# Pacing of indexed transfers, input and accumulator loads moved, and a reshuffled end of the last image

## The chip, the cores and the metric

The kernel runs on one core of a Trainium2 chip. The metric is device time in microseconds (us) of one execution. The engines are called as in the profile: PE is TensorE, DVE is VectorE, ACT is ScalarE, POOL is GpSimd, SP is SyncE (here it only issues DMAs).

## The reference, cut to what matters

The input is x of shape (4, 32, 128, 128). Layer 0 turns each image into 128 channels by 4096 positions. Layer 1 takes the result as 4096 tokens of 128 numbers per image.

```python
# layer 0, per image: q = xs is 128 channels (32 x 2 x 2) by 4096 positions
energy = einsum('bci,bcj->bij', q, q); d = sqrt(diagonal(energy))
attn = softmax(energy / (d_i * d_j))          # over positions
x = gamma * einsum('bcj,bij->bci', q, attn) + xs
# layer 1, on tokens t
t = t + linear_attention(layernorm(t))        # K^T V first, 8 heads
p = softmax(layernorm(t) @ router_w + router_b); top 2 of 8 experts, weights renormalised
t = t + sum over the two experts of weight * (layernorm(t) @ expert_w[e] + expert_b[e])
```

## The kernel before, in words

Four images (b = 0 to 3) go through one after another. The body of an image is `attend` (L387): for eight row chunks i of 512 positions and the chunks jc up to i, TensorE makes a 128x512 tile of energies (`pe`, L503), ScalarE takes its exponential and row sums (`pr`, L506), and TensorE multiplies it with the image into `po` (L410), two ticks later. The energy matrix is symmetric, so each tile off the diagonal serves twice: VectorE transposes it in 32x32 blocks (`F`, L361), SP stores it to DRAM (`blocks`, L453, 1 MB) and loads it back three ticks later with the blocks in place (`G`, L461, four loads), and TensorE multiplies it into `pg` (L367) when 57 units of work have passed; VectorE adds that to `o` (L377). For the last image's last row two tiles skip DRAM: 16 loads from F to G each (L446).

Beside the body of image b runs, in small steps, the rest: `prep` for image b + 1 (L278), `input_rows` for image b (L533, four loads of T from x per chunk, four chunks, on SP) and `layer1` for image b - 1 (L541). The lists `timed` and `steady` (L1213 to L1245) set the order: a `timed` entry has a begin and an end in per cent of the body's work, a `steady` one is advanced once for every 10 units of work. So one step of layer 1 comes about every three 128x512 products. Everything on PE, DVE, ACT and SP stays in the order in which the Python program emits it. What an engine waits for holds up everything after it on that engine.

In `layer1`, `close_rows` (L610) ends layer 0 for a quarter of the tokens (row sums, `pbd`, `df`, added into T), takes norm statistics, normalises into `xn` (ScalarE, L583, or VectorE, L666) and adds to the Gram matrix (`pgram`, L608). `matrix` (L684) turns the Gram matrix into one 128x136 matrix for attention (`pgv` L703, `pm` L711, `matx` L709). `attention_rows` (L791) applies it, stores the tokens to DRAM (t2) and routes. For images 0 to 2 `sorted_experts` (L832), once for each half h of the tokens, does the experts: GpSimd scatters tokens by expert with indexed DMAs (`xs`, L910), tiles of one expert are loaded (L933), transposed and multiplied (`pys`, L966 and L973), copied (L943 on ScalarE, L948 on VectorE) and stored (`ys`, L952); then GpSimd gathers two rows for each token (`yb`, L1028), and VectorE adds them, weighted (`combine`, L1000), into `acc`, which was loaded from t2 on SP (L1026), and `put` stores it (L1010). `acc` has three buffers of four token tiles. For image 2 five indexed transfers are issued in two steps, for images 0 and 1 four (L899, L918, L1033).

DMAs from SP and ACT also wait for the eighth DMA before them, since eight completion counters serve in turn.

The last image has no further body beside it. `first_parts` runs its `close_rows`, and `last_parts` (L1096) does the rest without sorting: all eight experts' products for each token tile k (`py`, L1107, two 128x512 products), VectorE adds some of the eight with the gate as weight (`scaled_sums`, L1055), ScalarE scales the others into `tmp` (`scaled_rows`, L1069), GpSimd sums these (`sum_rows`, L1076 to L1080), and `store` writes out. While the first half of the tokens goes through this, `second_half` (L1147) prepares the second half on the same engines, a piece at each k.

Of the kernel before, what the change touches and what calls it, by code (L numbers as in the profile page):

```python
# [22 lines left out]
def kernel(  # L23
# [156 lines left out]
    def idle(n):  # L180
        for _ in range(2 * n):
            yield

    held = []
    banks = [3]
# [92 lines left out]
    def prep(b, kc, st):  # L278
# [39 lines left out]
        for s in range(2):  # L318
# [8 lines left out]
            yield  # L327
        yield from idle(1)
        scaled = []
        for s in range(2):  # L330
# [56 lines left out]
    def attend(b, st):  # L387
# [11 lines left out]
        for i in range(NCH):  # L399
# [79 lines left out]
            for jc in order:  # L479
# [17 lines left out]
                for j in range(NJ):  # L497
                    t = NJ * jc + j
                    c0 = 0 if jc < i else P * j
                    yield  # L500
                    tick[0] += 1
                    pe = ps_e.tile([P, CH], F32, tag="pe", name=f"pe_{b}_{i}_{t}")
                    nc.tensor.matmul(pe[:, c0:], qn[jc][:, ts(j, P)], qn[i][:, c0:], start=True, stop=True)  # L503
                    pr = ppool.tile([P, CH], F32, tag="pr", name=f"pr_{b}_{i}_{t}")
                    exps[:] = [
                        nc.scalar.activation(pr[:, c0:], pe[:, c0:], AF.Exp, accum_out=sums[:, t, i : i + 1]).ins  # L506
                    ]
                    own.append(pr)
                    after(2, partial(values, pr[:, c0:], t, c0, CH))
                    if jc < i and not both:  # L510
                        after(1, partial(nc.vector.transpose, Fb[:, :, :, j, :], pr))
                        if j == NJ - 1:
                            after(2, partial(move, F, i, jc))
                    elif jc == i and j in (1, 2):

                        after(1 if j == 2 and order[-1] == i else 2, partial(below, own, (2, 1) if j == 1 else (3,)))
                    turn_tick()
                    clock[0] += 2 * (CH - c0) // P
                    step_share()
                    yield  # L520
# [20 lines left out]
    def layer1(b, st):  # L541
# [68 lines left out]
        def close_rows(kc):  # L610


            while len(st["o"]) < 2 * kc + 2 or any(st["got"][c] < NCH - 1 - c for c in (2 * kc, 2 * kc + 1)):
                yield from idle(1)
            late_rows = alone and kc >= 2
            while b > 0 and kc == 0 and not states[b - 1].get("sorted"):
# [28 lines left out]
            for j in range(NJ):  # L645
                nc.tensor.transpose(pb[:, ts(j, P)], wide[:, j].rearrange("p s c -> p (s c)"), ident)
            yield
            done()
            if not late_rows:
# [14 lines left out]
            if late_rows:  # L664
                for j in range(k + 4, k + 8):
                    nc.vector.tensor_scalar(  # L666
                        xn[:, j, :], T[:, j, :], rsa[:, j, :], nba[:, j, :], ALU.mult, ALU.add
                    )
            yield
            gram_rows(range(k, k + 4))  # L670
            yield
# [11 lines left out]

        def matrix(between=()):  # L684

# [20 lines left out]
            yield  # L706
            for f in between:
                f()
            pm, done = hold(f"pm_{b}", lambda p: nc.vector.tensor_copy(matx[:, : D + E], p[:, : D + E]))  # L709
# [122 lines left out]
        def sorted_experts(h):  # L832
# [65 lines left out]

            pause = (1, 4) if b == B - 2 else (1, 3)  # L899
            period = 5 if b == B - 2 else 4  # L900

            def offset(ap):
# [5 lines left out]
            for n in range(2 * HR):  # L908
# [9 lines left out]
                scatters.append(inst.ins)  # L918
                if n % period in pause:
                    yield  # L920
                    yield
# [75 lines left out]
            def combine(n):  # L997
# [5 lines left out]
                if k % 4 == 3 and i == 1:  # L1003
                    after_steps.append((now[0] + 2, partial(put, k // 4)))

            def put(g):
                for s in range(2):
                    for r1 in range(2):
                        p0 = s * 64 + r1 * 32
                        nc.sync.dma_start(dst_out[s, r1, :, ts(g, 4), :], accs[g][p0 : p0 + 32])  # L1010
# [11 lines left out]
            for n in range(2 * HR):  # L1022
                k, i = r0 + n // 2, n % 2
                if k % 4 == 0 and i == 0:
                    accs[k // 4] = work.tile([P, 4, D], F32, tag="acc", name=f"acc_{b}_{k // 4}", bufs=3)
                    nc.sync.dma_start(accs[k // 4], t2[:, ts(k // 4, 4)])  # L1026
                    yb[k // 4] = work.tile([P, 2, 4, D], F32, tag="wide", name=f"yb_{b}_{k // 4}")
# [3 lines left out]
                wait_for(pinned(inst).ins, exps, "not more of these at a time than steps have")  # L1031
                after_steps.append((now[0] + 3, partial(combine, n)))
                if n % period in pause:  # L1033
                    yield
                    yield
                    due()
# [23 lines left out]
        def scaled_rows(k, py, n=4):  # L1060

            if k % 2 == 0:
                nm = f"tmp_{b}_{k // 2}"
                if n == 4:
                    tmps[k // 2] = work.tile([P, 2, n, D], F32, tag="wide", name=nm)
# [8 lines left out]
        def sum_rows(kk, n=4, eng=nc.gpsimd):  # L1074
            tmp, rows = tmps[kk], accs[kk // 2][:, 2 * (kk % 2) : 2 * (kk % 2) + 2, :]
            eng.tensor_tensor(tmp[:, :, 0:2], tmp[:, :, 0:2], tmp[:, :, 2:4], ALU.add)  # L1076
            eng.tensor_tensor(tmp[:, :, 0], tmp[:, :, 0], tmp[:, :, 1], ALU.add)
            if n == 5:
                eng.tensor_tensor(rows, rows, tmp[:, :, 4], ALU.add)
            eng.tensor_tensor(rows, rows, tmp[:, :, 0], ALU.add)  # L1080
# [15 lines left out]
        def last_parts():  # L1096
# [3 lines left out]
            def bank(name):  # L1100
# [3 lines left out]
                return pool.tile([P, CH], F32, tag=tag, name=name)  # L1104

            def product(k, h, bank):
                nc.tensor.matmul(bank, xn[:, k, :], ew_sb[:, 4 * h : 4 * h + 4, :], start=True, stop=True)  # L1107
                return bank

            for _ in matrix([lambda g=g: transpose_rows(g)() for g in (6, 7)]):  # L1110
                pass

            la = fpool.tile([P, KT, 2 * E], F32, tag="F", name=f"la_{b}")
            copies = {}
            for u in range(4):
                if u >= 2:
                    copies[u] = fpool.tile([P, 8, D + 2 * E], F32, tag="F", name=f"pac_{b}_{u}")
                for j0 in range(0, 8, 3):
                    pa = bank(f"pat_{b}_{u}_{j0}")
                    attend_rows(u, j0, pa)  # L1120
                    if u < 2:
                        add_rows(u, j0, la[:, 8 * u : 8 * u + 8], pa)
                    else:
                        nj = min(3, 8 - j0)
                        nc.scalar.activation(
                            copies[u][:, j0 : j0 + nj].rearrange("p j d -> p (j d)"),
                            pa[:, : nj * (D + 2 * E)], AF.Copy,
                        )
            for u in (0, 1):
                bs, stats = batch_stats("f", 8 * u, 8)  # L1130
                for f in stats:
                    f()
                close_stats("f", 8 * u, 8, bs)
            logits = router_rows(nc.vector, 0, 16, la[:, :16])
            next(logits)
            normalise(range(0, 8), rsf, nbo)
            for _ in logits:
                pass
            gates = route(0)
            next(gates)  # L1140
            transpose_tokens(0)()
            transpose_tokens(1)()
            normalise(range(8, 16), rsf, nbo)
            for _ in gates:
                pass

            def second_half():  # L1147

                bs, stats = batch_stats("f", 16, 16)
                for u in (2, 3):  # L1150
                    tg = T[:, ts(u, 8), :]
                    nc.vector.tensor_tensor(tg, tg, copies[u][:, :, :D], ALU.add)
                    yield
# [4 lines left out]
                close_stats("f", 16, 16, bs)  # L1158
                for u in (2, 3):
                    nc.vector.tensor_copy(la[:, ts(u, 8)], copies[u][:, :, D:])  # L1160
                yield
                logits = router_rows(nc.vector, 16, 16, la[:, 16:])
                gates = None
                for g in range(4, 8):
                    normalise(range(4 * g, 4 * g + 4), rsf, nbo)
                    if g < 6:
                        next(logits, None)
                    else:
                        gates = gates or route(1)
                        next(gates, None)  # L1170
                    yield
                    transpose_tokens(g)()
                for _ in gates:
                    yield

            rest = second_half()
            products = [product(k, h, bank(f"py_{b}_{k}_{h}")) for k in range(2) for h in range(2)]
            transpose_tokens(2)()
            transpose_tokens(3)()
            for k in range(KT + 4):  # L1180
                if k < KT:
                    n = 5 if k < 16 else 4
                    scaled_sums(k, products[:2], 8 - n)
# [4 lines left out]
                if 1 <= k <= KT and k % 2 == 0:  # L1188
                    sum_rows(k // 2 - 1, 5 if k <= 16 else 4, nc.vector if k == KT else nc.gpsimd)
                if k >= 5 and k % 4 == 1:  # L1190
# [23 lines left out]
    for b in range(B):  # L1214
# [6 lines left out]
        if b + 1 < B:  # L1221
            nxt = states[b + 1]
            timed.append((prep(b + 1, 0, nxt), 66, 82, 12))
            timed.append((prep(b + 1, 1, nxt), 83, 99, 12))
        timed.append((input_rows(b, states[b]), 55, 75, 9))
        done = [0] * len(timed)
# [69 lines left out]
```

## Time and profile before

| | us |
|---|---|
| median of 3 runs (1788.23 to 1793.99) | 1790.51 |
| profiled execution, its own time | 1748.38 |
| its span, first to last instruction | 1746.6 |
| PE busy | 1666.0 |
| DVE busy | 878.6 |
| ACT busy | 929.6 |
| POOL busy | 509.2 |
| DMA | 330.81 MB, mean 189 GB/s |

All other times in this document's views come from the profiled execution and count from its first instruction. A wait line reads: engine and line that waited, what it waited for, us in total, number of times, longest. A timeline line reads: start, length, engine, line, operation, output<-input, count, and in brackets the idle time before it with what ended it; "x2" beside one 128x512 float32 product means its two passes, about 0.86 us together at the full clock. A window line reads: stretch, its length, busy time with the number of instructions, TensorE's granted clock (1 is full), share of the DMA engines, GB/s. The profile places the body of image 0 at about 0 to 400 us, image 1 at 400 to 800, image 2 at 800 to 1200 and image 3 at 1200 to 1637; the end of image 3 follows.

### The profile page before, as it was taken

How to read it: one execution, taken by the hardware profiler on the slowest of the kernel's cores; microseconds unless marked ns; L12 is line 12 of the kernel's file. 1: busy time of each engine (PE TensorE's matmuls, PEld its weight loads, DVE VectorE, ACT ScalarE, POOL GpSimd, SP SyncE). 2: the span in 40 equal slices, each digit the busy share in tenths (PEclk: the TensorE clock that was granted, in tenths of full speed). 3: DMA queues.
4: the chain of work that ended last, by engine and by line, in shares of the span. 5: the costliest groups of instructions: out<-in, count | busy, mean ns of one | idle time of the engine just before them, and what ended most of it. 6: DMA issues, size and time to landing. Idle time of an engine off the chain costs nothing. (4 is left out here: it accounts for less than half of the span.)

```text
span 1746.6 us, 20682 instructions
## 1 busy us (share of the span) xinstructions
PE 1666.0 (95%) x5580; PEld 891.6 (51%) x5580; DVE 878.6 (50%) x2213; ACT 929.6 (53%) x2875; POOL 509.2 (29%) x554
## 2 busy tenths in 40 slices
PE   7999999999999999989999999999999999989777
PEld 4544544455554556535564455544555455535533
DVE  3423333456385235556458334456647523444687
ACT  3555445465565545446565554545656554535376
POOL 1000000001026604651014630662101760562156
PEclk9999999999999999989999999999999999999999
DMA  2665788855657999884556889987555699984001
GB/s 63 169 186 164 214 210 246 234 162 145 178 156 217 256 247 258 251 246 114 148 170 198 247 236 254 267 251 199 145 156 170 209 271 256 271 253 108 1 13 37
DMA packets 217843, 330.81 MB, mean 189 GB/s; under 512 B 24448, under 2 KB 136576, under 8 KB 203776
## 3 DMA queue, kind: packets, MB, share of 16 engines
q1 hardware_dynamic: 200928, 296.82, 60.5%
q0 software_dynamic: 12288, 25.19, 5.0%
q10 hardware_dynamic: 4512, 7.48, 1.4%
q8 instruction: 46, 0.75, 0.2%
q14 instruction: 69, 0.57, 0.1%
HBM read 171.45 MB, written 160.96 MB: 190 GB/s over the span
## 5 line engine op out<-in xcount | busy, mean ns | idle before, releaser
L506 ACT ACTIVATE pr<-pe 128x512 f32<-128x512 f32 (+1 forms) x576 | 322.7, 560 | 553.9 <-PE pe L503 528.1
L410 PE MATMUL po<-pr,qT 128*128 128x512 f32 (+3 forms) x1152 | 550.4, 560 | 0.5 <-ACT o L415 0.5
L367 PE MATMUL pg<-G,qT 128*128 128x512 f32 x880 | 455.0, 599 | 25.4 <-DVE o L377 25.3
L503 PE MATMUL pe<-qn,qn 128*128 128x512 f32 x896 | 463.9, 600 | 1.8 <-ACT pr L506 1.8
L361 DVE STREAM_TRANSPOSE F<-pr 128x512 f32<-128x512 f32 x440 | 308.7, 704 | 196.8 <-ACT pr L506 195.0
L410 PEld LDWEIGHTS po<-pr,qT 128*128 128x128 f32 x1152 | 217.7, 191 | 243.7 <-issue 232.6
L372 ACT ACTIVATE junk<-G 128x512 bf16<-128x512 f32 x440 | 273.0, 620 | 0.0
L367 PEld LDWEIGHTS pg<-G,qT 128*128 128x128 f32 x880 | 162.8, 192 | 210.3 <-issue 156.9
L1028 POOL DMA_INDIRECT yb<-ys,place x192 | 185.0, 964 | 154.0 <-DMA ys<-xn 58.8
L910 POOL DMA_INDIRECT xs<-xn,place x192 | 185.9, 968 | 115.1 <-issue 39.0
L503 PEld LDWEIGHTS pe<-qn,qn 128*128 128x128 f32 x896 | 155.7, 192 | 117.4 <-issue 107.9
L377 DVE TENSOR_TENSOR o<-o,pg 128x512 f32<-128x512 f32 x110 | 75.1, 682 | 235.0 <-PE pg L367 234.7
L166 POOL TENSOR_TENSOR rn<-ss,neg_half 128x8 f32<-128x8 f32 (+1 forms) x17 | 26.8, 1578 | 459.7 <-DVE ss L321 401.4
L948 DVE COPY xn<-pys 128x256 f32<-128x256 f32 (+1 forms) x120 | 49.8, 416 | 187.1 <-ACT xn L943 106.3
L506 ACT ACTIVATION_READ_ACCUMULATOR pr<-pe 128x1 f32 x576 | 111.9, 194 | 0.0
L943 ACT ACTIVATE xn<-pys 128x256 f32<-128x256 f32 (+1 forms) x120 | 44.7, 377 | 115.2 <-PE pys L973 114.2
L1000 DVE SCALAR_TENSOR_TENSOR acc<-yb,weight,acc 128x128 f32<-128x128 f32 x192 | 64.7, 342 | 71.7 <-DMA yb<-ys,place 40.1
L166 POOL TENSOR_TENSOR rsf<-dm_f,neg_half 128x8 f32<-128x8 f32 (+1 forms) x15 | 26.1, 1743 | 255.0 <-DVE sv_f L575 255.0
L966 PEld LDWEIGHTS pys<-ew_sb,xn 128*128 128x128 f32 x468 | 69.8, 193 | 56.6 <-issue 45.1
L503 PE MATMUL pe<-qn 128*128 128x512 f32 (+3 forms) x256 | 91.4, 439 | 0.7 <-ACT qn L338 0.7
L166 POOL TENSOR_TENSOR rsa<-dm_a,neg_half 128x8 f32<-128x8 f32 x16 | 26.3, 1644 | 220.7 <-DVE sv_a L575 220.7
L372 ACT ACTIVATION_READ_ACCUMULATOR junk<-G 128x1 f32 x440 | 84.5, 192 | 0.0
(178 smaller groups left out, 1550.1 us busy)
## 6 DMA issues: line engine op xcount, KB each, us to landing
blocks<-F SPq DMA_DIRECT2D x108, 1024.0 KB
G<-blocks SPq DMA_DIRECT2D x432, 256.0 KB
xn<-xs SPq DMA_DIRECT2D x114, 128.0 KB
ys<-xn SPq DMA_DIRECT2D x114, 128.0 KB
T<-in_x_dram SPq DMA_DIRECT2D x64, 128.0 KB
out_dram<-acc SPq DMA_DIRECT2D x128, 64.0 KB
xx<-in_x_dram SPq DMA_DIRECT2D x62, 128.0 KB
t<-T SPq DMA_DIRECT2D x12, 512.0 KB
```

The costliest lines, as they stand in the source:

```text
L166: pinned(nc.gpsimd.tensor_tensor(dst, src, neg_half.to_broadcast(list(src.shape)), ALU.pow))
L361: f()
L367: nc.tensor.matmul(pg.rearrange("p (a f) -> p a f", a=4), st["qT"][i][:, ib, :], G[:, :, ib], start=(ib == 0), stop=(ib == NJ - 1),)
L372: nc.scalar.activation(junk, G[:, :, ib], AF.Copy, accum_out=st["sums"][:, NJ * i + ib, jc : jc + 1])
L377: nc.vector.tensor_tensor(o, o, pg.rearrange("p (a j c) -> p a j c", a=4, c=S), ALU.add)
L410: nc.tensor.matmul(row["po"][:, lo:hi], qT[blk // NJ][:, blk % NJ, :], w, start=start, stop=(row["left"] == 0))
L503: nc.tensor.matmul(pe[:, c0:], qn[jc][:, ts(j, P)], qn[i][:, c0:], start=True, stop=True)
L506: nc.scalar.activation(pr[:, c0:], pe[:, c0:], AF.Exp, accum_out=sums[:, t, i : i + 1]).ins
L910: inst = nc.gpsimd.indirect_dma_start(xs[h], offset(place[:, i, k : k + 1]), xn[:, k, :], None)
L966: nc.tensor.matmul(p[:, 2 * P + j * D : 2 * P + j * D + D], bufs[4 + g % 2][:, j, :], weights[:, bass.ds(begins[2 * (g % 2) + j], D)], sta ...
L1000: nc.vector.scalar_tensor_tensor(a[:, k % 4, :], yb[k // 4][:, i, k % 4, :], weight[:, i, k, :], a[:, k % 4, :], ALU.mult, ALU.add)
L1028: inst = nc.gpsimd.indirect_dma_start(yb[k // 4][:, i, k % 4, :], None, ys, offset(place[:, i, k : k + 1]))
```

## The change

1. `keep_running` issues transposes of the identity into a spare bank, whose result nobody reads: 22 at the first `prep`, 36 before the last quarter's Gram products, 6 before the first token transposes of the end.
2. In `sorted_experts` two indexed transfers are issued in each step for every image; images 0 and 1 had that already.
3. The load of `acc` goes from SP's queue to ACT's and is issued one step later; `combine` comes four steps after its gather instead of three.
4. `input_rows` of images 1 and 2 runs at 82 to 99 per cent of the body instead of 55 to 75.
5. The end of the last image: the last `close_rows` emits its row-sum work when the last exponential has been emitted, so that its `pbd` transposes come before the last `po` product; its Gram products are emitted in the order k, k+4, k+1, k+5 and so on; `transpose_rows` of groups 6 and 7 moves from before `pm` to after the first `pat`; statistics of the first eight tiles come before the second `pat`; ScalarE copies the logits' part `la`; the second half's first pieces come before the first gate; ScalarE takes 6 of the 8 scaled products for k under 8, 5 for k under 14, then 4 (before: 5 for k under 16, then 4), and the `tmp` tiles of 6 and 5 come from the pool of G with three buffers.

```diff
+    def keep_running(n, pool=None, tag=None):
+        bank = psum_t("spare") if pool is None else pool.tile([P, CH], F32, tag=tag, name="spare")
+        for _ in range(n):
+            nc.tensor.transpose(bank[:, :P], ident, ident)
...
         yield from idle(1)
+        if first:
+            keep_running(22, ps_y, "py")
         scaled = []
...
+            while "exps" not in st if last_rows else missing():
                 yield from idle(1)
...
                 nc.tensor.transpose(pb[:, ts(j, P)], wide[:, j].rearrange("p s c -> p (s c)"), ident)
             yield
+            while missing():
+                yield from idle(1)
             done()
...
+            if last_rows:
+                keep_running(36)
+                gram_rows([k + j // 2 + 4 * (j % 2) for j in range(8)])
+                yield
+                return
             gram_rows(range(k, k + 4))
...
-            pause = (1, 4) if b == B - 2 else (1, 3)
-            period = 5 if b == B - 2 else 4
...
-                if n % period in pause:
+                if n % 2:
                     yield
                     yield
...
+            def fetch(g):
+                nc.scalar.dma_start(accs[g], t2[:, ts(g, 4)])
...
-                    nc.sync.dma_start(accs[k // 4], t2[:, ts(k // 4, 4)])
+                    after_steps.append((now[0] + 1, partial(fetch, k // 4)))
...
-                after_steps.append((now[0] + 3, partial(combine, n)))
-                if n % period in pause:
+                after_steps.append((now[0] + 4, partial(combine, n)))
+                if n % 2:
...
-            eng.tensor_tensor(tmp[:, :, 0:2], tmp[:, :, 0:2], tmp[:, :, 2:4], ALU.add)
+            m = n // 2
+            eng.tensor_tensor(tmp[:, :, :m], tmp[:, :, :m], tmp[:, :, m : 2 * m], ALU.add)
...
+            def by_scalar(k):
+                return 6 if k < 8 else 5 if k < 14 else 4
...
-            for _ in matrix([lambda g=g: transpose_rows(g)() for g in (6, 7)]):
+            for _ in matrix():
                 pass
...
+            attended(0)
+            stats_of(0)
+            transpose_rows(6)()
+            transpose_rows(7)()
+            attended(1)
+            stats_of(1)
+            attended(2)
+            attended(3)
...
+            logits = router_rows(nc.vector, 0, 16, la[:, :16])
+            next(logits)
+            normalise(range(0, 4), rsf, nbo)
+            keep_running(6)
+            transpose_tokens(0)()
+            next(rest)
+            for _ in logits:
+                pass
+            gates = route(0)
+            normalise(range(4, 8), rsf, nbo)
+            next(gates)
+            next(rest)
+            for _ in gates:
+                pass
             products = [product(k, h, bank(f"py_{b}_{k}_{h}")) for k in range(2) for h in range(2)]
+            transpose_tokens(1)()
+            normalise(range(8, 16), rsf, nbo)
             transpose_tokens(2)()
             transpose_tokens(3)()
...
-        timed.append((input_rows(b, states[b]), 55, 75, 9))
+        timed.append((input_rows(b, states[b]), *((55, 75) if b in (0, B - 1) else (82, 99)), 9))
```

## The prediction

> **What bounds the kernel now.** I read the busy table, then TensorE's waits, then the stretches in which those waits lie, then VectorE's and SP's timeline there.
>
> ```profile
> PE 1666.0 (95%) x5580; PEld 891.6 (51%) x5580; DVE 878.6 (50%) x2213; ACT 929.6 (53%) x2875; POOL 509.2 (29%) x554
> PE pg L367 <- DVE o L377: 25.3, 13, 6.2
> PE pgram L608 <- ACT xn L583: 8.6, 2, 8.3
> PE pys L966 <- DVE xn L948: 8.3, 3, 4.0
> PE py L1107 <- ACT tmp L1069: 8.1, 5, 1.9
> PE ptn L340 <- DVE qs L332: 8.0, 3, 4.6
> ```
>
> TensorE is busy 1666.0 of 1746.6 us, and the change takes no matmul of use away. Only its 80.6 us of waits, and the slow clock that follows long ones, are for sale. TensorE waits for VectorE, though VectorE is half idle; so I looked at what VectorE waits for.
>
> ```profile
> 648.91 0.42 DVE L948 COPY xn<-pys 128x256 f32<-128x256 f32 x1 [9.18 <-DMA ys<-xn]
> 649.39 1.22 PE L966 MATMUL pys<-ew_sb,xn 128*128 x4 [4.04 <-DVE xn L948]
> ...
> 764.00 0.74 DVE L1000 SCALAR_TENSOR_TENSOR acc<-yb,weight,acc 128x128 f32<-128x128 f32 x2 [5.97 <-DMA acc<-t]
> 772.23 2.08 PE L367 MATMUL pg<-G,qT 128*128 128x512 f32 x2 [6.24 <-DVE o L377]
> ...
> 753.08 1.75 SPq L461 DMA_DIRECT2D G<-blocks  x4
> 754.92 1.86 SPq L1010 DMA_DIRECT2D out_dram<-acc  x4
> 756.99 0.34 SPq L1026 DMA_DIRECT2D acc<-t  x1
> ```
>
> Image 1's body holds two stalls. At 649 a copy waits for a ys store while the DMA engines run at a share of 1.0 to 1.2. At 764 VectorE waits for acc, which SP issued last, behind 1 MB of G and 256 KB of stores. Image 2's body repeats both (4.0 us at 1068, 6.5 us in 1100:1200). Image 3's has 9.7 us in 1450:1600, where VectorE waits 23.6 us for gathers (yb) and 24.3 us for ys stores.
>
> ```profile
> 1641.50:1642.00 0.50, 0.00 (x0) 0.87 0.00 0
> 1648.50:1649.00 0.50, 0.50 (x5) 0.80 0.00 0
> 1645.74 3.45 PE L608 MATMUL pgram<-xn 128*128 128x128 f32 x16 [8.28 <-ACT xn L583]
> ```
>
> These show TensorE's clock (last-but-two column) halve at 1641.9 in the 8.28 us wait and return at 1648.7, so 16 matmuls took 3.45 us where the 16 at 1633 took 1.95.
>
> **What the Trainium skill says.** (1) TensorE: Matmul & The Clock Gate, Part 1: activity is judged in free-running windows of about 3.4 us. The trace agrees: 1641.9, 1648.7, 1665.7 and 1672.6 lie whole multiples of 3.41 apart; a window about 77% busy (648.6 to 652.0) did not raise the clock, one 38% busy (764.7 to 768.1) lowered it. (2) The same page, Part 4, says that transposes don't engage the fast clock; no stretch of this trace is of transposes alone for a whole window, so it is open. (3) DMA: Bandwidth & Descriptors, Queues, rings and completion order: an engine turns between the rings of SP and ACT packet by packet, so a transfer on ACT's ring needn't sit out SP's backlog. No row here has acc on ACT. (4) SBUF — State Buffer, SBUF: two separate sides: a GpSimd operation and a VectorE one with two SBUF inputs shut each other out. It agrees: 128x128 router operations take 0.29 us alone and 0.70 to 1.39 beside GpSimd's sums (1693 to 1697).
>
> **The change, part by part.** A stall is priced as its wait plus half of the slow-clock time in which TensorE then worked.
>
> *T loads of images 1 and 2, from 55–75 to 82–99 per cent of the body.* They take 2.1 MB per image (about 8.4 us at the 250 GB/s of that stretch) and 16 SP issues out of 600 to 650. Stakes: 4.0 + 6.0/2 = 7.0 us (image 1), 4.0 + 3.3/2 = 5.7 (image 2). I take 10 of 12.7. They land in 730 to 775, before T is first read at 768.7, but that stretch already moves 242 GB/s: see below.
>
> *acc load on ScalarE's queue, a step later; combine a step later.* Distance load to use stays three steps. What goes is the place behind G and the stores: issue to landing was about 7 us (756.99 to 763.9). Stakes: 7.9 + 6.1/2 = 10.9 (image 1, 700:800), 6.5 + 3.2/2 = 8.1 (image 2). I take 13 of 19. What it adds: 24 issues on ScalarE of about 0.46 us (row of L204 at 2.2 us), hidden in its 1.28 us idle per step; and a wait. The load reuses the buffer of three groups before, so ScalarE, in order, waits for that group's stores, with the exponentials behind it, and TensorE behind those. Stores are issued four steps (4 x 2.58 = 10.3 us) before. They now follow a 1 MB blocks store, so they land perhaps 9 to 10 us after. TensorE's second next pe needs the exponential, so about 3.4 us of ScalarE delay is covered. The T loads delay G in the same place by 2 us a chunk. For both together I take 2 us loss per image, 4 in images 1 and 2 (bounds 0 and 15).
>
> *Two transfers per step for image 2.* One gather costs GpSimd 0.94 + 0.30 = 1.25 us, so 2.5 per step need 3.1 us where a step has 2.58; two need 2.5, which fits. Image 3's stakes are 9.7 + 3.5/2 = 11.4. The ys part remains, since image 3's T loads stay at 55–75: I take 5.5 (bounds 0 and 11.4). The phase ends later: 64 steps instead of 51, that is 33 us, with gathers until about 1605, where VectorE still has idle pieces of 7 to 8 us; cost nothing, at most 2 if that cover is gone. But stores of groups 3 and 4 now follow, on SP, the two rows of 16 G loads (13.4 and 10.9 us). I follow ScalarE's loads for groups 6 and 7: each waits about 5 us, less 3.4 covered; the second meets a ScalarE with normalising to do. I take 4 lost (bounds 0 and 9).
>
> *22 transposes at the start.* They fill 7.75 to 12.4, in which TensorE waits anyway; all slow they take 22 x 0.213 = 4.7 us, so at most 0.15 us late. If they raise the clock, the first ptn, pe and ptn save 0.45 + 1.05 + 0.45 = 2.0. Both ends kept; I take 1.5.
>
> *The end.* (a) pbd before the last po: df starts after o at about 1634.6 instead of 1636.54: 1.9. (b) 36 transposes (3.9 us) before the gram: if they count, up to 1.5 us of slow clock goes; if not, the earlier start gives 1 back: take 0.75. (c) ptx 6 and 7 leave the way of pm: 0.65. (d) From the first pat to the finished gate: 18.2 us before. After, counted through the new order (pat_0 adds, 8 statistics, close, 2.25 of GpSimd, second eight, router, the added T add of 1.22 and 4 statistics of 0.86, 14 route operations): 19.1. Loss 0.9, with 2.1 us of later VectorE work done. (e) From the gate to VectorE's end: 69.4 before. TensorE's floor is 30 x 1.72 + 7 x 0.43 = 54.6. VectorE gives six products to ScalarE; for k under 14 VectorE then has 29 us, ScalarE 31 (78 x 0.28, 4 normalisings of 1.65, 4 evictions), GpSimd 30, with a sum of 768 elements estimated at 1.9 us from 1.27 for 512. With three buffers for tmp this leaves about 39 us to k = 17, then 14 x 1.72 = 24, and 3.3 of closing: 67, gain 2.4. Sum 1.9 + 0.75 + 0.65 - 0.9 + 2.4 = 4.8 (bounds 0 and 8).
>
> **Sum:** 10 + 13 - 4 + 5.5 - 4 + 1.5 + 4.8 = 26.8 us off the profiled 1748.4 (span 1746.6 and 1.8 around it), to 1721.6. The median, 1790.51, lies 42 us above that execution; its extra time is not on the page, so I carry the gain over in us: 1763.7, say 1764.
>
> **Rivals.**
> - *Crowding eats the second gain.* The T loads join a stretch at 242 of some 260 GB/s; acc is prompt, but G and blocks are late, VectorE waits again. For: share about 1.0 for most of 740 to 790. Against: some 13 us of free DMA time in 740:800. Then the 13 goes: 1777.
> - *All stalls go*, being one chain that fed itself, and the end gains 8: 12.7 + 19 + 11.4 + 2 + 8 less about 8 of ScalarE's waits = 45: 1745.
> - *Slower: ScalarE waits for stores at each of 24 loads.* Without it the gain is about 35. It decides from 35/24 = 1.5 us a load beyond the 3.4 covered, a mean wait of 4.9 us. At 6 us: 24 x 2.6 = 62 lost, net 27 slower: 1818; at 5.2 us about 1799.
> - *It does nothing:* stalls move to the next DMA wait, transposes don't count, the end evens out: 1790.
>
> **Chances.** Forecast (1754 to 1770) 0.47, crowding (to 1785) 0.22, all stalls 0.15, nothing 0.07, slower 0.09. A measurement tells 0.3% (5.4 us) from no change. Faster 0.84, same 0.07, slower 0.09. The range 1740 to 1787 leaves out the slower case and the far end of the third.
>
> **What would show it.** Right: no wait of VectorE for acc on 700:800 and 1100:1200; no 9 us wait for ys near 649 and 1066; few yb waits after 1540; PE waits under pg L367 below 12 us; clock 1.0 from about 10.3 us and at the last gram. Wrong: ScalarE idle before an exponential on acc or stores; G named before pg; slow clock through the transposes.

## The result and the profile after

| | before | changed |
|---|---|---|
| median of 4 runs, side by side, us | 1792.25 (1788.23 to 1794.64) | 1767.69 (1764.09 to 1771.84) |
| profiled execution, its own time, us | 1748.38 | 1771.84 |

The ratio is 0.9866, interval 0.9836 to 0.9896: 24.6 us faster, where 26.8 were forecast. A set here is a group of runs timed side by side. The two profiles can't be subtracted: before has a median of 1751 us in two sets (its profile shown above is of that kind) and of 1790 to 1800 in the others, even on one chip, so each comparison below is made inside one set, with the time of before in that set beside it. Three single executions of the third set, 2514 to 5167 us long, are left out of its ratios.

TensorE's busy line of the changed kernel:

```profile
PE 1681.7 (95%) x5644; PEld 896.6 (51%) x5644; DVE 878.2 (50%) x2199; ACT 928.2 (52%) x2893; POOL 510.3 (29%) x553
```

64 transposes are new in it (5644 - 5580). Its `pg` products, with the idle time before them (34.8 us, 11.0 of it ended by VectorE's `o`), and some of its waits (us in total, times, longest):

```profile
L375 PE MATMUL pg<-G,qT 128*128 128x512 f32 x880 | 454.6, 598 | 34.8 <-DVE o L385 11.0
...
PE pg L375 <- DVE o L385: 11.0, 6, 3.7
PE pg L375 <- DMA G<-blocks: 10.3, 6, 3.1
...
PE pe L511 <- ACT pr L514: 7.5, 12, 1.9
...
PE pe L511 <- ACT pr_back L495: 2.5, 1, 2.5
```

And VectorE's:

```profile
DVE xn L965 <- DMA ys<-xn: 111.0, 33, 7.2
...
DVE acc L1017 <- DMA yb<-ys,place: 16.7, 10, 2.9
DVE acc L1017 <- DMA acc<-t: 15.7, 5, 4.2
```

TensorE's wait for VectorE's `o` is 11.0 us, against 25.3 in the profile of before, but all waits before `pg` are 34.8 us, against 25.4 there: G, which was not named there, accounts for 10.3. ScalarE stands before the energies for 10.0 us (1.8 there). The reason for the latter is seen on ScalarE at 740 (start, length, engine, line, operation; in brackets the idle time):

```profile
740.67 0.62 ACT L380 ACTIVATE junk<-G 128x512 bf16<-128x512 f32 x1
741.19 0.19 ACT L380 ACTIVATION_READ_ACCUMULATOR junk<-G 128x1 f32 x1
751.14 0.37 ACTq L1024 DMA_DIRECT2D acc<-t  x1
751.62 0.60 ACT L514 ACTIVATE pr<-pe 128x512 f32<-128x512 f32 x1 [10.24 <-DMA out_dram<-acc]
```

ScalarE ends at 741.38, issues the acc load only at 751.14, and the exponential waits behind it: 9.8 us for stores of the group three before, whose buffer it reuses (the counters of these four stores are among those it waits for, and the last of them is full at 750.97). Measured so on ScalarE's timeline (issue less the end of its instruction before), 8 of the 24 loads wait, 60.7 us in all: the last three in the body of image 1, the last three in that of image 2, and the last two in that of image 3.

The start and the last Gram products, first before's start:

```profile
12.38 1.11 PE L340 MATMUL ptn<-ident,qs 128*128 128x128 f32 x4 [4.63 <-DVE qs L332]
```

```profile
7.46 3.64 PE L188 MATMUL spare<-ident 128*128 128x128 f32 x22
12.29 0.66 PE L348 MATMUL ptn<-ident,qs 128*128 128x128 f32 x4 [1.20 <-DVE qs L340]
...
1667.00 4.14 PE L188 MATMUL spare<-ident 128*128 128x128 f32 x36
1672.06 2.05 PE L618 MATMUL pgram<-xn 128*128 128x128 f32 x16 [0.92 <-ACT xn L593]
```

The four transposes took 1.11 us before, the 16 products 3.45: behind spare transposes TensorE runs at its fast clock. At the start nothing but transposes had run on TensorE by 12.29: the first spare ones take 0.21 us each, as the eight `ptq` before them do, and the 22 together 3.64 instead of the 4.7 of a slow clock throughout.

### The profile page after: what moved, and what is told of

Same layout as the page of the kernel before. It is cut to its first block, busy times and chain, and to the rows that moved or that the text cites. A ratio compares the mean times of both kernels' runs of the same rounds, so it can differ in the third digit from the quotient of the medians.

```text
span 1770.1 us, 20808 instructions
## 1 busy us (share of the span) xinstructions
PE 1681.7 (95%) x5644; PEld 896.6 (51%) x5644; DVE 878.2 (50%) x2199; ACT 928.2 (52%) x2893; POOL 510.3 (29%) x553
## 5 line engine op out<-in xcount | busy, mean ns | idle before, releaser
L375 PE MATMUL pg<-G,qT 128*128 128x512 f32 x880 | 454.6, 598 | 34.8 <-DVE o L385 11.0
L927 POOL DMA_INDIRECT xs<-xn,place x192 | 186.0, 969 | 138.9 <-ACT pr L514 50.5
L166 POOL TENSOR_TENSOR rn<-ss,neg_half 128x8 f32<-128x8 f32 (+1 forms) x17 | 26.8, 1578 | 450.6 <-DVE ss L327 392.4
```

The lines of the kernel that those rows point to most:

```text
L166: pinned(nc.gpsimd.tensor_tensor(dst, src, neg_half.to_broadcast(list(src.shape)), ALU.pow))
L375: nc.tensor.matmul(pg.rearrange("p (a f) -> p a f", a=4), st["qT"][i][:, ib, :], G[:, :, ib], start=(ib == 0), stop=(ib == NJ - 1),)
L927: inst = nc.gpsimd.indirect_dma_start(xs[h], offset(place[:, i, k : k + 1]), xn[:, k, :], None)
```

## The experiments

An edit is shown against the kernel that it changes. "Alone" means before plus one part; "without" means the changed kernel minus one part.

**First set, where before took 1750.74 us (31 runs).** Before again, to see which kind its profile was:

> The kernel before, unchanged, profiled once more, because its first profiled execution (1748.4 us) lay 42 us below its timed median (1790.5). If that execution was the rare one, this one takes about 1790 us and its profile shows where the 42 us go: as longer waits of TensorE for VectorE's o in the bodies of images 1 and 2 (late G or late acc) if they are DMA waits that fall differently from execution to execution; as a lower granted clock everywhere if not. If a profile as such makes the execution faster, it takes about 1748 us again.

1750.08 us, with the waits of the first profile (26.8 us before pg). So the forecast's stalls were read from a usual execution of this kind; where the other 42 us go, it can't show.

T moved, alone:

```diff
-        timed.append((input_rows(b, states[b]), 55, 75, 9))
+        timed.append((input_rows(b, states[b]), *((55, 75) if b in (0, B - 1) else (82, 99)), 9))
```

> The kernel before with only the loads of T for images 1 and 2 moved to 82 to 99 per cent of the body. The forecast's sum gives 10 us off (stakes 12.7), so about 1780 us against 1790. The crowding rival: the loads now meet an acc load that still stands behind G and stores on SP, the stretch at 700 to 800 grows what the one at 600 to 650 saves, and the time stays within 3 us of before or rises.

1754.83 us, ratio 1.0031 (1.0018 to 1.0044): 4.1 slower. Two stretches, first before, then with T moved (length, TensorE's busy time, its clock, DMA share, GB/s):

```profile
600.00:650.00 50.00, 46.28 (x176) 1.00 0.97 251
700.00:750.00 50.00, 49.29 (x144) 1.00 0.93 267
```

```profile
600.00:650.00 50.00, 48.43 (x182) 1.00 0.83 224
700.00:750.00 50.00, 43.80 (x121) 0.93 0.98 251
```

The stall at 649 shrinks, 2.2 us of TensorE's time; at 700 to 750, where the DMA engines were at 0.93 already, 5.5 us are lost. In image 2, 2.0 us are won at 1050 to 1100 and 1.2 lost at 1150 to 1200. The crowding rival had it right, by way of image 1.

The acc load on ScalarE's queue, one step later, with the combine one step later, alone:

```diff
-                    nc.sync.dma_start(accs[k // 4], t2[:, ts(k // 4, 4)])
+                    after_steps.append((now[0] + 1, partial(fetch, k // 4)))
...
-                after_steps.append((now[0] + 3, partial(combine, n)))
+                after_steps.append((now[0] + 4, partial(combine, n)))
```

> The kernel before with only the acc load moved to ACT's queue and one step later, the combine one step later as well. The forecast gives 13 us off less up to 2 for ScalarE's waits on stores (images 1 and 2), so 11 us off, about 1779. The rival in which ScalarE waits for stores at each load gives a time above 1790, with ScalarE named before pe.

1746.60 us, ratio 0.9979 (0.9968 to 0.9989): 4.1 faster. VectorE's 23.0 us of waits that name acc are gone (12.3 us in five waits before the same instruction, at most 4.3, name nothing), so a transfer on ScalarE's ring passes SP's backlog, as the Trainium skill has it (DMA: Bandwidth & Descriptors, Queues, rings and completion order). But 11 of ScalarE's 24 loads wait, 64.2 us in all, and TensorE waits 16.4 us for ScalarE's exponentials. The stall changed its engine.

Two transfers per step for image 2, alone:

```diff
-            pause = (1, 4) if b == B - 2 else (1, 3)
-            period = 5 if b == B - 2 else 4
...
-                if n % period in pause:
+                if n % 2:
```

> The kernel before with only image 2's transfers by index slowed from five to four in two steps. The forecast gives 5.5 us off for the gathers that VectorE waits for in image 3's body, without ScalarE's waits here since acc is still loaded on SP: about 1785. The 'does nothing' rival: stalls move to other waits, within 2 us of before.

1760.24 us, ratio 1.0055 (1.0039 to 1.0072): 9.5 slower, neither theory. SP and VectorE late in image 3's body:

```profile
1568.24 12.89 SPq L446 DMA_DIRECT2D G<-F  x16
...
1583.29 0.44 SPq L1023 DMA_DIRECT2D acc<-t  x1
1583.88 10.01 SPq L446 DMA_DIRECT2D G<-F  x16
```

```profile
1569.76 0.76 DVE L997 SCALAR_TENSOR_TENSOR acc<-yb,weight,acc 128x128 f32<-128x128 f32 x2 [7.65 <-issue]
1587.36 0.74 DVE L997 SCALAR_TENSOR_TENSOR acc<-yb,weight,acc 128x128 f32<-128x128 f32 x2 [10.50 <-DMA G<-F]
```

The later gathers push the acc load of 1583.29 behind the first 16 G loads of the last row, and VectorE's wait of 10.50 us ends 4 us after its issue; that it is this load which ends it, and not the G load that the trace names, is inferred. The wait of 7.65 us has no named cause; the acc load before it was issued at 1563.22, ahead of those G loads. The forecast named this place, but had ScalarE pay there.

**Second set, where before took 1799.51 us (40 runs).** The changed kernel again:

> The changed kernel, unchanged, beside a kernel before that takes either about 1750 us, as in the first experiments and in the profile that the forecast was worked from, or about 1790, as in the runs that it was measured against. If the changed kernel gains from what is the same in both cases (start, end, order of transfers), it is again about 25 us below before: 1725 or 1767. If what it removes is a wait that only the 1790 case has (slower transfers), it gains nothing beside a 1750 before, or loses: the parts that ran alone there, plus 4, minus 4 and plus 9.5, give 1750 + 9.5 less 6 for start and end = about 1754.

1774.93 us, ratio 0.9873 (0.9845 to 0.9902): 24.6 faster, as in the first comparison. The first set's parts don't add up to that.

The end alone (part 5 with its 36 and 6 transposes):

> The kernel before with only the new end of the last image (with its 36 and 6 transposes), the body and the start as before. The forecast's terms give 4.8 us off (0 to 8): 1746 beside 1750.7, or 1786 beside 1790.5. If ScalarE and GpSimd become late with the six products (a rival price of that term), no gain: within 2 us of before.

1795.07 us, ratio 0.9974 (0.9960 to 0.9988): 4.4 off, 4.8 forecast. Its body is that of before, so it also shows what before does where it takes 1800. The same place in both sets, first before in the first set, then this kernel:

```profile
577.38 0.96 POOL L910 DMA_INDIRECT xs<-xn,place  x1 [0.30 <-issue]
...
578.64 0.96 POOL L910 DMA_INDIRECT xs<-xn,place  x1 [0.30 <-ACT junk L372]
...
578.73 0.69 DVE L377 TENSOR_TENSOR o<-o,pg 128x512 f32<-128x512 f32 x1 [2.86 <-PE pg L367]
...
579.59 0.60 ACT L506 ACTIVATE pr<-pe 128x512 f32<-128x512 f32 x1 [1.28 <-PE pe L503]
```

```profile
579.02 0.96 POOL L928 DMA_INDIRECT xs<-xn,place  x1 [0.30 <-issue]
...
580.28 0.95 POOL L928 DMA_INDIRECT xs<-xn,place  x1 [0.30 <-issue]
...
583.48 0.69 DVE L383 TENSOR_TENSOR o<-o,pg 128x512 f32<-128x512 f32 x1 [7.59 <-remote]
...
583.53 0.60 ACT L512 ACTIVATE pr<-pe 128x512 f32<-128x512 f32 x1 [5.19 <-remote]
```

In both GpSimd issues transfers by index back to back, with 0.30 us between them: a train. In the first set ScalarE and VectorE work on beside it; in the second both stand still, with a releaser that the view doesn't know ("issue", "remote"), and go on 2.3 us after the train's last transfer ends at 581.23. I added up such gaps of over 0.3 us: 3.2 us on ScalarE and none on VectorE for before in the first set, 140.6 and 106.6 here. 69 of ScalarE's 82 and 36 of VectorE's 40 end while GpSimd issues such transfers or within 1 us after. The sums take whole gaps; some of them, such as 1.28 us between two exponentials, are as long in the first set and only lack their releaser here. From 622 to 679, where GpSimd issues none and the DMA engines have a share of 0.94, there is no such gap.

What they wait for can be found in the trace's semaphore records (a semaphore is a counter that an engine raises when an instruction ends, and for which others wait). At 583.5 both wait for the counter that only TensorE raises. Its records come at 583.46, 583.50 and 583.55, the first since 574.44, though the products that raise it ended, by the trace, at 576.15, 577.00, 578.72, 579.58 and 580.44. All 15 waits over 1.5 us that are called "remote" in this run end within 0.02 us of such a record, 1.8 to 8.2 us after the last TensorE instruction that raises the counter. For 261 of the 458 such instructions that end in a train of two or more, or up to 2.5 us after it, no record follows within 0.12 us; elsewhere it lacks for 1 of 1117. For before in the first set it is 4 of 467 and none of 1100. Three products of 0.86 us each can't have ended within 0.09 us. So in these waits TensorE has done its work and its signal shows late; where a record is only missing, as at 577.00, the waiting engine can go on in time.

The waits from which the forecast was priced look different in this kind of set. For VectorE here and in the changed kernel of this set they are 12.4 and 15.4 us for gathers, 9.1 and 12.0 for acc (and 26.4 and 5.3 before the same instruction with nothing named), 50.5 and 88.0 for ys stores; for TensorE's products behind VectorE's `o`, 20.9 and 14.4.

Without the pacing of image 2 (five in two steps again):

> The changed kernel with image 2's transfers by index back at five in two steps. Alone the slower pace cost 9.5 us where the forecast has a gain. If that cost is the pace's own (stores and gathers of image 2 run 33 us later and meet the end of image 3), this kernel is 8 to 10 us faster than the changed one. If it came from acc loads on SP standing behind the G loads of the last row, which the changed kernel has on ACT's queue, this kernel is no faster than the changed one.

1791.85 us, ratio 0.9957 (0.9943 to 0.9971). The pacing is worth 16.9 us here, where alone in the first set it cost 9.5. This kernel's longest trains of image 2 have 20, 16, 15 and 13 transfers, the changed kernel's 12. Over 1320 to 1680 us the unexplained gaps of ScalarE and VectorE add up to 98.1 us here and to 66.4 in the changed kernel. Two other causes are too small: ScalarE's acc loads in image 3's body wait 14.9 and 13.7 us, and VectorE's gathers after 1480 only 3.7 and 0.

Without the move of T:

> The changed kernel with T of images 1 and 2 loaded at 55 to 75 per cent again. The forecast's price of the move is 10 us, so this kernel would be 10 us slower than the changed one. The crowding rival: the move costs more in 700 to 800 and 1100 to 1200 than it saves (alone it cost 4 us), so this kernel is 0 to 5 us faster, and TensorE's waits under pg for G disappear.

1765.35 us, ratio 0.9816 (0.9790 to 0.9842): 9.6 faster than the changed kernel. TensorE's waits for G are gone (6.4 us in the changed kernel of this set), and ScalarE's acc loads wait 31.8 us in all instead of 55.8. The load that waited 9.8 us above:

```profile
743.02 0.19 ACT L380 ACTIVATION_READ_ACCUMULATOR junk<-G 128x1 f32 x1
748.20 0.36 ACTq L1024 DMA_DIRECT2D acc<-t  x1
```

It waits 5.0 us here and 9.5 in the changed kernel of this set. So the moved T loads delay the stores for which ScalarE waits.

**Third set, where before took 1790.41 us.**

> The changed kernel again, as the measure for the two runs beside it. Before took about 1751 us in the first experiments and about 1800 in the second. If before takes about 1800 here, this kernel takes about 1775 (25 below, as twice so far). If before takes about 1751, the parts measured alone there (plus 4, minus 4, plus 9.5) with 6 to 7 off for start and end add up to about 1754: no gain.

1764.31 us, ratio 0.9857 (0.9829 to 0.9885).

Without the new place of the acc load (the diff of the acc load above, reversed):

> The changed kernel with the acc load back on SP's queue, at its old step, and the combine three steps after its gather. The forecast prices the move at 13 us off less 4 to 8 for ScalarE's waits on stores, so this kernel should be 5 to 9 us slower than the changed one, with VectorE waiting for acc again. Alone the move was worth 4 us. The rival, that ScalarE's waits eat the gain, makes it no slower than the changed kernel.

1775.09 us, ratio 0.9920 (0.9891 to 0.9948): 10.8 slower than the changed kernel, above the 5 to 9 expected. VectorE waits 28.9 us for acc again, and 27.6 us of TensorE's waits are for VectorE.

T not moved, and a slower pace for images 0 and 1:

```diff
-                if n % 2:
+                if n % 2 if b == B - 2 else n % 3 < 2:
```

> The changed kernel with T of images 1 and 2 at 55 to 75 per cent again (1765 us beside an 1800 before), and with three transfers by index per two steps instead of four for images 0 and 1. Theory: where before takes 1800, VectorE and ScalarE stand still, for no reason that the trace names, while GpSimd issues six or more indexed transfers back to back; three per two steps fill 3.8 us of about 5.2, so such trains vanish for images 0 and 1, about two thirds of the unexplained idle time (111 us on each of the two engines) goes with them, and the kernel is 8 to 15 us faster than 1765. Rival: the idle time belongs to the number of transfers and not to their trains; then it is only spread out, the phases end about 60 us later and the time is 1765 or worse. Where before takes 1751, there is no such idle time and both expect no gain.

1740.41 us, ratio 0.9716 (0.9688 to 0.9745), the best against its before. From 0.9816 (second set) to 0.9716 are some 18 us, more than the 8 to 15 expected. Over 500 to 1320 us, with the transfers of images 0 and 1, the unexplained gaps of both engines fall from 139.3 us (without the move of T) to 50.5; over 1320 to 1680, with image 2's unchanged pace, from 79.8 to 75.9. The number of transfers is the same, 384, so the idle time is not a price per transfer. The gain is not all of that, though: ScalarE's acc loads wait 6.6 us in all instead of 31.8, since at a slower pace the stores are done in time. One long train is left, 22 gathers of image 2:

```profile
1574.88 0.95 POOL L1048 DMA_INDIRECT yb<-ys,place  x1 [0.30 <-issue]
1577.50 0.60 ACT L495 ACTIVATE pr_back<-pe_back 128x512 f32<-128x512 f32 x1 [14.88 <-issue]
...
1578.24 2.07 PE L493 MATMUL pe_back<-qn,qn 128*128 128x512 f32 x2 [11.43 <-issue]
```

ScalarE goes on 1.7 us after its end at 1575.83, and TensorE has stood idle for 11.43 us.

**Fourth set, where before took 1751.31 us.** Image 2's gathers also wait for the exponentials of the tiles that skip DRAM:

```diff
-                    nc.scalar.activation(pr, pe, AF.Exp, accum_out=sums[:, NJ * i + j, jc : jc + 1])
+                    exps[:] = [
+                        nc.scalar.activation(pr, pe, AF.Exp, accum_out=sums[:, NJ * i + j, jc : jc + 1]).ins
+                    ]
```

> The kernel of the run before (T of images 1 and 2 at 55 to 75 per cent, three transfers by index per two steps for images 0 and 1), and in addition image 2's gathers wait for the exponentials of the two tiles of the last row that skip DRAM as well (pr_back); so far these don't count, and 22 gathers go out back to back at 1548 to 1576 us while ScalarE stands still for 14.9 us until 1.7 us after the last of them. Theory that such trains hold up ScalarE and VectorE: the train falls apart into pairs, the standstill of 14.9 us and TensorE's wait of 11.4 us go, some 3 us come back because the last gathers end later, and the time is 6 to 11 us below the kernel of the run before, whose ratio to before was 0.972: a ratio of about 0.967. Rival, that the standstill has another cause and only happens to end with the train: it stays, and the ratio stays at 0.972. If before takes about 1751 us here instead of 1790, ScalarE doesn't stand still in trains; then the last edit brings nothing, and what is seen is whether the three edits beat before there: start and end are worth 6 us, the loads on ScalarE's queue 4, so a ratio of about 0.995.

1733.61 us, ratio 0.9890 (0.9870 to 0.9910); 0.995 was expected for such a set. Here no trace shows standstills in trains, so this gain of 17.7 us has another source, which no run isolates. So these edits beat before here too, and without the last one they beat both kernels where before takes 1790 (1740.41 against 1764.31 and 1790.41). Its last edit stays untested: the train has still 20 gathers, since a pair takes 2.5 us of a step of 2.58, and ScalarE has no unexplained gaps in this set (3.2 us, as before). What is left is the wait that the forecast placed here:

```profile
1576.41 0.34 ACTq L1026 DMA_DIRECT2D acc<-t  x1
1576.85 0.60 ACT L496 ACTIVATE pr_back<-pe_back 128x512 f32<-128x512 f32 x1 [10.37 <-DMA out_dram<-acc]
```

## Why the prediction was right, and where it was not

Sign and size came out (1764 against 1767.7), but by luck: two large errors cancel. The measured column holds the 1790 to 1800 sets, each part taken out of the changed kernel, the end put in alone, the start read from the trace. The parts act on each other, so that their sum meets the 24.6 us measured is no proof of each of them:

| step of the sum | forecast, us | measured, us |
|---|---|---|
| T loads of images 1 and 2 | +10 | -9.6 |
| acc load, less ScalarE's waits in the bodies of images 1 and 2, and of image 3 | +13 - 4 - 4 | +10.8 |
| image 2's pace | +5.5 | +16.9 |
| 22 transposes | +1.5 | +2.0 |
| the end | +4.8 | +4.4 |
| sum | 26.8 | 24.5 |

- *T loads: wrong in sign.* The step "I take 10 of 12.7" counted what leaves 600 to 650 and charged the arrival, into a stretch "at 242 of some 260 GB/s", with 2 us a chunk inside another term. Alone it gained 2.2 us of TensorE's time at 600 to 650 and lost 5.5 at 700 to 750. In the changed kernel it delays G, and the stores for which ScalarE's acc loads wait (24 us more of such waits). The forecast's sign that VectorE's 9 us waits for ys would go came true by the letter only: the longest is 7.2 us, but one of 6.9 still stands at 646. Other signs failed in the changed kernel's first profile: VectorE waits for acc for 6.3 us at 700 to 800 and for 5.3 at 1100 to 1200, and the waits before `pg` are 34.8 us, not below 12. Two of the signs of being wrong were there: G before `pg`, and ScalarE idle before an exponential on stores.
- *acc load: right in mechanism, its net gain put too low.* VectorE's wait for acc became ScalarE's wait for stores. The forecast charged image 3's share of these waits to the pace, but they belong to the load: without the pacing they are as long (14.9 us, 13.7 with it). The forecast thought of about 5 us per load in image 3's body; measured are 7.3 and 7.2 there, and 5.1 to 9.8 for the last three loads in the bodies of images 1 and 2. The slower rival's mechanism is thus real: its decisive mean of 4.9 us over 24 loads was 60.7/24 = 2.5.
- *Image 2's pace: right in sign in the changed kernel, but mis-sized by 11.4 us, and not by the mechanism that was priced.* It was priced from VectorE's waits for gathers in a profile of the 1748 kind (23.6 us at 1450 to 1600); where it gains, the trace without it has only 3.7 us of them. (The sign for this term came true: the changed kernel has none after 1540.) Alone, in the 1748 kind of set, it costs 9.5: an acc load fell between the rows of 16 G loads, and the bound for the later end ("at most 2 if that cover is gone") did not hold. In the changed kernel, where before takes 1800, it gains 16.9, and the trace shows shorter trains and 31.7 us less of unexplained gaps beside it. That this is how it gains was not tried by itself; the slower pace for images 0 and 1 speaks for it. Nor does any run separate the kind of set from the kernel around the pacing: with acc on ScalarE's queue, no acc load stands behind the G loads on SP.
- *Start: right.* The first po product begins at 16.11 instead of 18.10 (18.87 and 17.78 in two other traces with before's start, 16.12 and 16.19 in two more of the changed kernel). These transposes do raise the clock, the question that was left open.
- *End: right as a sum.* From the trace: the last Gram products start 8.5 us after the last po product instead of 12.3 (forecast 1.9 off, measured 3.9, the pbd transposes now standing ahead of that product); they take 2.05 instead of 3.45 us (0.75 forecast, 1.4); pgv to pat 4.3 instead of 5.2 (0.65, 0.9); first pat to the first gated sum 18.10 instead of 18.24 (0.9 lost forecast, 0.1 gained); from there to VectorE's end 69.0 instead of 69.4 (2.4, 0.4). These add up to 6.7; timed are 4.4, interval 2.2 to 7.2. The last is the weak one: giving ScalarE six products hardly shortened the whole.
- *"I carry the gain over in us"* held only by that cancelling. The page of before could not show that its other executions lose their 42 us beside GpSimd's trains.

Open: why signals come late beside trains in some sets and not in others. All timed executions were traced at least for their span and clock, so that the tracing takes part in it is not excluded. Open too is the changed kernel beside a before of 1751. The separate parts there, 4.1 - 4.1 + 9.5, less 4.4 and 2.0 from elsewhere, add up to 3 us slower; that is an estimate and was not run, and for the last kernel a sum of this kind gave 0.995 where 0.989 was measured.

## What to carry to other kernels

Moving a load out of a crowded stretch gains only if the stretch that takes it has room: price the arrival as carefully as the departure. A load put on a working engine's queue turns a wait of its consumer into a wait of that engine, so first make the buffer's last use old enough; here a slower pace for the transfers around it did that. And take a part out of the finished kernel as well as putting it in alone, in more than one set of runs: the same pacing was worth +16.9 us in one kernel and set and -9.5 in another.

## What the runs showed of the hardware that was not expected

- These float32 transposes count for TensorE's clock. The Trainium skill says that transposes don't (TensorE: Matmul & The Clock Gate, Part 4); here four transposes behind 22 spare ones, with nothing but transposes before them, took 0.66 us instead of 1.11, and 16 products behind 36 took 2.05 instead of 3.45. The measurement decides for these; the trace records them as matmuls and doesn't show whether they run in the mode of which the page speaks.
- While GpSimd issues transfers by index back to back, ScalarE and VectorE can stand still for up to 14.9 and 15.2 us. Where the semaphore records tell, they wait for TensorE's signal, which shows 1.8 to 8.2 us after its work (second set, the end alone). Of the seven waits of ScalarE over 4 us that overlap such a train in the third set's changed kernel, acc loads left out, six end 1.8 to 2.3 us after its last transfer. In the stretch shown, TensorE works on until 580.44 and then waits for VectorE's `o`. In other sets before has trains of up to 54 transfers and shows nothing of it.
- One program took 1746 to 1756 us in one set of runs and 1792 to 1807 in the next on the same chip; the first 500 us were alike, and from 812 to 890, where neither trace has a train, the distance between the traces of before (first set) and of the end alone (second set) stays at 12.8 us.
